# Layer 2 of a sparse graph kernel: row tiles 12 to 20 take two node tiles whole instead of six, and four others through a second list of two chunks

## The chip, the cores and the metric

The kernel runs on one core of a Trainium2 chip. A core has a matrix engine (TensorE, PE in the profile), a vector engine (VectorE, DVE), a scalar engine (ScalarE, ACT), GpSimd (POOL), a queue engine that issues most transfers (SyncE, SP), and 16 DMA engines between its memory (SBUF) and HBM. Each engine works through its own instructions in a fixed order and waits for others by semaphores. The metric is the device time of one execution in microseconds (us); the median of several executions is compared.

## The reference

Four layers over a graph of 2708 nodes with 512 features; `adj` is a 2708 x 2708 matrix of floats, most of them zero. Each layer normalizes x, and its result is added to x. Cut to what matters here, layer 2 is:

```python
h = jnp.maximum(_layernorm(x, axis=-1), 0.0)
h = jax.nn.relu(adj @ (h @ W1) + b1)      # first pass over adj
h = jax.nn.relu(adj @ (h @ W3) + b3)      # second pass over adj
x = x + jnp.tanh(h @ Wf + bf)
```

Layer 0 and layer 3 also multiply by matrices made from `adj`. The nodes are drawn so that the first ones have most neighbours: the probability of an entry falls with the square root of both indices. The inputs have a fixed seed.

## The kernel before, in words

The nodes are cut into 22 tiles of 128 (NT = 22; the last has 20). A row tile m is 128 rows of `adj`. Its columns are taken in two ways. The six first node tiles (DENSE = 6, 768 columns, where nearly every column is used) are multiplied whole. Of the other columns only those that have an entry in some row of m are multiplied: layer 0 counts them, finds their indices with a search (line 377) and stores the indices in `idx_g` and the gathered columns of `adj` in `listed[m]` in HBM, in CHUNKS[m] chunks of 128. Row tiles 12 to 20 have 6, 6, 6, 5, 6, 5, 5, 5 and 5 chunks. Row tile 0 has none; it takes all columns whole.

Layer 2 goes twice through all row tiles, in the loops at lines 1039 (first pass, source g1d in HBM) and 1208 (second pass, source g2d, where tile 0 comes first, then 6 to 20 with the last tile among them, then 1 to 5). For each row tile, `aggregate` (line 905) accumulates in two PSUM banks:

- For the whole tiles it loads three node tiles of `adj` at a time (`load_piece`), splits each piece into a high part (ACT, line 933), a low part and a mixed part (DVE, 934 and 935), and multiplies each node tile in three fast products (line 946) with parts of the features that stay in SBUF.
- For the list it loads `listed[m]` (line 890, two buffers) and gathers the features of each chunk with an indirect transfer from GpSimd (line 897) into one of eight buffers gg0 to gg7, used in turn. Each chunk is one product in full FP32 (line 949), which the engine runs as two passes.
- In the first pass ACT also marks the nonzero entries of whole and listed columns for layer 3 (line 915).

The sum goes through ACT and DVE (lines 823, 824, 974), is transposed on PE (837), split (842, 843, 846) and multiplied by a weight matrix (862). In the first pass the result `go` is stored to g2d; the second pass has a longer tail with tanh, a norm and a second weight product.

The order in which the instructions stand on each engine is fixed by a scheduler before the run; the program's text gives priorities and buffers. Tiles named `slot0` to `slot19` hold x and y while row tile 0 makes its products in the first pass, and the loaded g2 while it does so in the second. Weight banks, `a_hi`, `a_lo`, `a_s` and `ac` have two buffers each.

Of the kernel before, what the change touches and what calls it, by code (L numbers as in the profile page):

```python
# [9 lines left out]
FP = mybir.dt.float32  # L10
# [12 lines left out]
P = 128  # L23
# [12 lines left out]

DENSE = 6
LEAD = 3
CHUNKS = (0, 10, 9, 8, 7, 7, 7, 7, 6, 6, 6, 6, 6, 6, 6, 5, 6, 5, 5, 5, 5, 2)


@with_exitstack
def kernel(
# [43 lines left out]
    def rows(t):  # L87
        return min(P, N - t * P)
# [37 lines left out]
    BEHIND = DENSE * P  # L126
    WIDE, LOW = (N - BEHIND) // 4, BEHIND // 2
    assert WIDE * 4 == N - BEHIND and WIDE < BLK and LOW * 2 == BEHIND
    cnt_b = dram.tile([NGROUP, P, WIDE], BF, name="cnt_b")
    cnt_l = dram.tile([NGROUP, P, LOW], BF, name="cnt_l")  # L130

# [2 lines left out]

    idx = const.tile([P, NT], U32, name="idx")
    BAD_BOUND, BAD_NEG, BAD_MANY = NT, NT + 1, 2 * NT + 1
    bad = const.tile([P, 3 * NT + 1], FP, name="bad")
    nc.gpsimd.memset(bad, 0.0)
    flag = const.tile([P, 1], I32, name="flag")

# [1 line left out]
    idx_g = const.tile([P, NT, NCH], U32, name="idx_g")  # L142

    rdeg = const.tile([P, NT], FP, name="rdeg")
    ones_b = const.tile([P, 1], BF, name="ones_b")
    nc.gpsimd.memset(ones_b, 1.0)

# [69 lines left out]
    with tc.tile_pool(name="l0_slab", bufs=2) as slabs, tc.tile_pool(  # L217
# [29 lines left out]
        nc.gpsimd.iota(place_i, pattern=[[P, NCH]], base=1, channel_multiplier=1)  # L247
        places = hp.tile([P, NCH], FP, name="places")
        nc.vector.tensor_copy(places, place_i)

        pending, pending_c = [], []

# [547 lines left out]
    NGG = 8  # L800
# [12 lines left out]
    NMARK = DENSE + NCA  # L813
    gather_slot = [0]

    def gathered():
        name = f"gg{gather_slot[0] % NGG}"
        gather_slot[0] += 1
        return gp.tile([P, D], FP, name=name)

    def sum_banks(dst, main, mixed, n):

# [63 lines left out]
        return raw[:k, : len(ts), :n], k  # L886

    def load_listed(m):
        ac = ap.tile([P, NCA, P], FP, name="ac")[:, : CHUNKS[m], : rows(m)]
        nc.sync.dma_start(out=ac, in_=listed[m])  # L890
        return ac

    def gather(m, gd, gs=None, index=idx_g):

# [10 lines left out]
    def aggregate(m, parts, shifted, gd, marked):  # L905


        n = rows(m)
        whole, num = dense_of(m), CHUNKS[m]
        if marked:  # L910
            nz = ap.tile([P, NMARK, P], U8, name="nz", bufs=3)

            def mark(i, a):
                k, ts = a.shape[:2]
                nc.scalar.activation(nz[:k, i : i + ts, :n], a, AF.Sign)
        main = ps_a.tile([P, D], FP, name="agg") if dense_of(m) else None
        mixed = ps_a.tile([P, D], FP, name="aggs")
        chunks = []
        if num:
            ac = load_listed(m)  # L920
            chunks = [(ac[:, c, :], g) for c, g in enumerate(gather(m, gd))]
            if marked:
                mark(whole, ac)
        for ts in dense if dense_of(m) else []:
            gs = [parts(t) for t in ts]
            raw, k = load_piece(m, ts)
            hi, lo, s = (
                ap.tile([P, PIECE, P], FR, name=f"a_{part}") for part in ("hi", "lo", "s")
            )
            d = (slice(0, k), slice(0, len(ts)), slice(0, n))  # L930
            if marked:
                mark(ts[0], raw)
            nc.scalar.activation(hi[d], raw, AF.Copy, scale=UP)  # L933
            nc.vector.tensor_tensor(lo[d], raw, hi[d].bitcast(FP), ALU.subtract)  # L934
            nc.vector.scalar_tensor_tensor(
                s[d], lo[d].bitcast(FP), SHIFT, hi[d].bitcast(FP), op0=ALU.mult, op1=ALU.add
            )
            for i, t in enumerate(ts):
                ghi, glo, gs_ = gs[i]
                first, last = t == 0, t == DENSE - 1  # L940
                for acc, a, b, st, sp in (
                    (main, hi, ghi, first, False),
                    (main, lo, glo, False, last),
                    (mixed, s, gs_, first, False),
                ):
                    nc.tensor.matmul(acc[:n], a[:k, i, :n], b[:k], start=st, stop=sp)  # L946
        if chunks:
            for c, (a, g) in enumerate(chunks):
                nc.tensor.matmul(  # L949
                    mixed[:n],  # L950
                    a,
                    g,
                    start=(c == 0 and not dense_of(m)),
                    stop=(c == len(chunks) - 1),
                )
        else:
            for ts in others:
                gs = [shifted(t) for t in ts]
                raw, k = load_piece(m, ts)
                for i, t in enumerate(ts):  # L960
                    nc.tensor.matmul(
                        mixed[:n], raw[:, i, :], gs[i][:k], start=False, stop=(t == NT - 1)
                    )
        if marked:
            nc.sync.dma_start(out=nonzero[m], in_=nz[:, : whole + num, :n])
        return main, mixed
# [69 lines left out]
    w3 = split_w(wsetb, wr, "wb")  # L1036
    wr = load_w(wset, wf_d, "wr")

    for m in order_m:
        n = rows(m)  # L1040
        parts = aggregated(m, first_parts, first_product, g1d, bias1, marked=True)
        if m == 0:
            wf = split_w(wset, wr, "wa")
# [163 lines left out]
    FIRST = 2  # L1207
    for m in order_2:
        n = rows(m)
        parts = aggregated(m, second_parts, second_product, g2d, bias3)  # L1210
        if m == 0:
            w = split_w(wsetb, wr, "wb")
# [499 lines left out]
```

## Time and profile before

| | |
|---|---|
| median of 9 runs | 1487.31 us (1481.0 to 1492.78) |
| profiled execution | 1489.11 us, span of the profile 1487.3 us |
| mean granted PE clock | 0.94 |
| layer 2, list products of line 949 | first at 646.2 us, last at 1269.6 us |
| whole products, line 946 | 3 groups of 252, mean 457, 405 and 401 ns |
| list passes, line 949 | 520, mean 597 ns |
| gathers, line 897 | 130 in each pass, mean 1023 and 1008 ns |
| DMA | 351.27 MB, 236 GB/s over the span |

Times of matmuls are from start to an estimated end and overlap when they follow each other closely; the spacing of their starts is what they cost. Idle time of an engine is given with what ended it. In a row of a timeline the columns are start, duration, engine, line, operation, output and inputs, count, and in brackets the idle time before it. A wait names who waited, for whom, total us, times, and the longest.

### The profile page before, as it was taken

The page shows a single profiled execution, that of the slowest core. Times are in us where ns is not written, and L with a number is a line of the kernel's source. Part 1 is how long each engine was busy: PE and PEld are TensorE (multiplying, and loading weights), DVE is VectorE, ACT ScalarE, POOL GpSimd, SP SyncE. Part 2 cuts the span into 40 slices and gives each one's busy share as a digit, 9 for nine tenths or more (in the row PEclk, how much of TensorE's full clock was granted, in tenths as well). Part 3 has the DMA queues.
Part 4 walks back from the last instruction along what each step waited for, and adds up shares of the span by engine and source line. Part 5 has one row for each costly group of instructions (what it writes and reads, how often), then busy time and mean ns, then how long its engine had stood idle before and what let it go on. Part 6 is the DMA issues. An engine that isn't in the chain of part 4 may idle for free. (4 is left out here: it accounts for less than half of the span.)

```text
span 1487.3 us, 15398 instructions
## 1 busy us (share of the span) xinstructions
PE 1306.7 (88%) x4400; PEld 771.2 (52%) x4400; DVE 939.5 (63%) x1888; ACT 676.4 (45%) x1040; POOL 672.8 (45%) x690
## 2 busy tenths in 40 slices
PE   6487889789778769999999999899999999768997
PEld 2133434334333246655656666565676666556664
DVE  2577879779879679543344446465666665565574
ACT  5987555374111256432333334254445444454453
POOL 1172657667553332055544441234324345157762
PEclk9698989999889879999999999999999999889998
DMA  8998989997786597377777777756555666377884
GB/s 294 307 344 289 332 286 308 311 288 219 224 327 227 147 319 242 103 232 259 247 239 223 235 223 236 240 155 200 178 170 161 210 195 204 102 259 247 263 260 144
DMA packets 195940, 351.27 MB, mean 236 GB/s; under 512 B 26444, under 2 KB 107692, under 8 KB 192113
## 3 DMA queue, kind: packets, MB, share of 16 engines
q1 hardware_dynamic: 148453, 200.68, 40.5%
q0 software_dynamic: 47392, 149.51, 32.3%
q8 instruction: 37, 0.61, 0.2%
q14 instruction: 58, 0.48, 0.1%
HBM read 286.99 MB, written 63.12 MB: 235 GB/s over the span
## 5 line engine op out<-in xcount | busy, mean ns | idle before, releaser
L949 PE MATMUL aggs<-gg,ac 128*128 128x512 f32 (+1 forms) x520 | 233.7, 597 | 3.8 <-DMA gg<-g1d,idx_g 3.8
L897 POOL DMA_INDIRECT gg<-g2d,idx_g x130 | 131.0, 1008 | 218.7 <-PE aggs L949 169.8
L897 POOL DMA_INDIRECT gg<-g1d,idx_g x130 | 133.0, 1023 | 174.9 <-PE aggs L949 104.4
L741 PE MATMUL acc<-h,inc 128*128 128x512 f32 x348 | 165.7, 618 | 29.4 <-DVE inc L600 26.3
L532 POOL DMA_INDIRECT ac<-in_adj_t_dram,idx_a x130 | 131.6, 1012 | 85.2 <-issue 32.3
L949 PEld LDWEIGHTS aggs<-gg,ac 128*128 128x128 f32 (+1 forms) x520 | 98.0, 190 | 111.5 <-issue 102.5
L550 POOL DMA_INDIRECT h<-h0d,idx_g x111 | 113.4, 1021 | 89.9 <-PE acc L741 62.9
L741 PEld LDWEIGHTS acc<-h,inc 128*128 128x128 f32 x348 | 64.8, 196 | 108.1 <-issue 67.8
L946 PE MATMUL agg<-ghi,a_hi 128*128 128x512 f32 x252 | 115.2, 457 | 5.0 <-ACT a_hi L933 4.7
L933 ACT ACTIVATE a_hi<-raw 128x384 fp32r<-128x384 f32 x84 | 43.5, 519 | 161.5 <-issue 89.0
L741 PE MATMUL acc<-h,incl 128*128 128x512 f32 (+1 forms) x222 | 105.2, 620 | 0.0
L946 PE MATMUL agg<-glo,a_lo 128*128 128x512 f32 x252 | 102.1, 405 | 1.8 <-ACT glo L200 1.8
L946 PE MATMUL aggs<-gs,a_s 128*128 128x512 f32 x252 | 100.3, 401 | 0.7 <-DVE gs L197 0.6
L897 POOL DMA_INDIRECT gg<-hidr,idx_h x79 | 78.2, 990 | 46.0 <-PE agg L1133 15.5
L934 DVE TENSOR_TENSOR a_lo<-raw,a_hi 128x384 fp32r<-128x384 f32 x84 | 47.2, 562 | 79.9 <-ACT a_hi L933 53.6
L157 PE MATMUL yacc<-wvo,hT 128*128 128x512 f32 (+1 forms) x176 | 87.3, 642 | 3.9 <-ACT hT L186 3.8
L843 DVE SCALAR_TENSOR_TENSOR v_lo<-pt,v_hi 128x512 fp32r<-128x512 f32 (+1 forms) x88 | 56.7, 664 | 46.5 <-ACT v_hi L842 45.9
L824 DVE SCALAR_TENSOR_TENSOR u<-aggs,u 128x512 f32<-128x512 f32 x42 | 28.8, 687 | 77.5 <-PE aggs L949 75.9
L741 PEld LDWEIGHTS acc<-h,incl 128*128 128x128 f32 (+1 forms) x222 | 43.6, 200 | 53.8 <-issue 50.1
L483 ACT ACTIVATE sgn<-ar 128x2708 bf16<-128x2708 f32 (+1 forms) x22 | 54.0, 2455 | 36.1 <-DMA ar<-in_adj_dram 35.5
L842 ACT ACTIVATE v_hi<-pt 128x512 fp32r<-128x512 f32 (+1 forms) x88 | 48.8, 578 | 44.5 <-PE pt L837 42.6
L514 DVE FIND_INDEX8 at_top<-top,ar 128x8 uint32<-128x2708 f32 (+1 forms) x22 | 65.3, 2969 | 0.0
(275 smaller groups left out, 2776.9 us busy)
## 6 DMA issues: line engine op xcount, KB each, us to landing
ar<-in_adj_dram SPq DMA_DIRECT2D x27, 1354.0 KB
raw<-in_adj_t_dram SPq DMA_DIRECT2D x108, 192.0 KB
slot<-x SPq DMA_DIRECT2D x41, 256.0 KB
at<-in_adj_t_dram SPq DMA_DIRECT2D x27, 384.0 KB
ranks<-rank_b SPq DMA_DIRECT2D x20, 485.0 KB
ac<-lst SPq DMA_DIRECT2D x16, 384.0 KB
h<-in_x_dram SPq DMA_DIRECT2D x21, 256.0 KB
h0d<-h POOLq DMA_DIRECT2D x21, 256.0 KB, 7.1
```

The lines of the kernel that those rows point to most:

```text
L157: nc.tensor.matmul(acc[:n], hT[:, c, :n], w[:, c, :], start=(c == 0), stop=(c == NCD - 1))
L483: nc.scalar.activation(sgn[:n], ar[:n], AF.Sign, accum_out=sum_sgn[:n])
L514: nc.vector.max_index(at_top[:n], top[:n], ar[:n])
L532: nc.gpsimd.indirect_dma_start(out=ac[:, c, :n], out_offset=None, in_=adj_units, in_offset=bass.IndirectOffsetOnAxis(ap=idx_a[:, m, c0 + c ...
L550: nc.gpsimd.indirect_dma_start(out=g, out_offset=None, in_=h0d[:, :], in_offset=bass.IndirectOffsetOnAxis(ap=idx_g[:, m, c : c + 1], axis=0),)
L741: nc.tensor.matmul(acc[:n], a, g, start=(i == 0), stop=(i == len(pairs) - 1))
L842: nc.scalar.activation(hi[d], pt[d], AF.Relu, scale=UP)
L843: nc.vector.scalar_tensor_tensor(lo[d], pt[d], 0.0, hi[d].bitcast(FP), op0=ALU.max, op1=ALU.subtract)
L897: nc.gpsimd.indirect_dma_start(out=gs[c], out_offset=None, in_=gd[:, :], in_offset=bass.IndirectOffsetOnAxis(ap=index[:, m, c : c + 1], ax ...
L934: nc.vector.tensor_tensor(lo[d], raw, hi[d].bitcast(FP), ALU.subtract)
L946: nc.tensor.matmul(acc[:n], a[:k, i, :n], b[:k], start=st, stop=sp)
L949: nc.tensor.matmul(mixed[:n], a, g, start=(c == 0 and not dense_of(m)), stop=(c == len(chunks) - 1),)
```

## The change

For row tiles 12 to 20 (`is_sparse`), in both passes, only node tiles 0 and 1 are multiplied whole (FEW = 2). The columns of node tiles 2 to 5 (512 of them) are searched for those that are used, and taken as two more chunks (FEW_CHUNKS = 2). The columns of `adj` for these chunks are gathered straight from the transposed input into the free end of the `ac` tile, twice, once in each pass; with the two gathers of features that makes four more transfers from GpSimd per row tile and pass.

The search runs in the first pass: `few_ranks` once, before row tile 4, makes running counts for nine row tiles from the counts of layer 0, and `few_search` for row tile m runs in the iteration of row tile m - 6. Its indices go to unused places in `idx_g`. If more than 256 columns are used, a flag leads to the general path, as with the other list.

The first pass still loads all six whole tiles, because it marks them for layer 3; the second pass does not load what it does not use. Gathered features may use slot1 to slot4 besides gg0 to gg7: in the first pass from row tile 1 on, in the second for row tiles from 6 on.

```diff
+SPARSE, FEW, FEW_CHUNKS = 12, 2, 2
...
+    rank_f = dram.tile([NT, (DENSE - FEW) * P], HF, name="rank_f")
...
+        nc.vector.tensor_copy(places_f, places[:, :8])
...
+    more_places = [[]]
+
     def gathered():
-        name = f"gg{gather_slot[0] % NGG}"
+        names = [f"gg{i}" for i in range(NGG)] + more_places[0]
+        name = names[gather_slot[0] % len(names)]
         gather_slot[0] += 1
         return gp.tile([P, D], FP, name=name)
...
+    FEW_A, FEW_G = max(CHUNKS[SPARSE:]), max(CHUNKS[SPARSE:]) + FEW_CHUNKS
+    BETWEEN = (DENSE - FEW) * P
...
+    def is_sparse(m):
+        return SPARSE <= m < NFULL
+
+    def few_ranks():
+        r = NFULL - SPARSE
+        total, rank = (
+            ap.tile([P, PIECE, P], FR, name=f"a_{part}").rearrange("p t k -> p (t k)").bitcast(to)
+            for part, to in (("hi", BF), ("lo", HF))
+        )
+        for g in range(r // GROUP):
+            nc.sync.dma_start(
+                out=total[g * GROUP : (g + 1) * GROUP, : DENSE * P].rearrange(
...
+        rank = rank[:r, :BETWEEN]
+        nc.vector.tensor_scalar_min(rank, total[:r, FEW * P : DENSE * P], 1.0)
+        nc.vector.tensor_tensor_scan(rank, rank, rank, 0.0, ALU.add, ALU.max)
+        nc.sync.dma_start(out=rank_f[SPARSE:NFULL], in_=rank)
+
+    def few_search(m):
+        ranks = ap.tile([P, PIECE, P], FR, name="a_s").rearrange("p t k -> p (t k)").bitcast(HF)
+        nc.sync.dma_start(
+            out=ranks[:, :BETWEEN], in_=rank_f[m : m + 1].to_broadcast([P, BETWEEN])
+        )
...
+        nc.vector.tensor_scalar_add(end, ranks[:, BETWEEN - 1 : BETWEEN], 1.0)
+        nc.vector.tensor_copy(ranks[:, BETWEEN:], end)
+        nc.vector.tensor_scalar(want, places_f, end, None, op0=ALU.min)
+        nc.vector.max_index(at, want, ranks)
...
     def load_listed(m):
-        ac = ap.tile([P, NCA, P], FP, name="ac")[:, : CHUNKS[m], : rows(m)]
-        nc.sync.dma_start(out=ac, in_=listed[m])
-        return ac
+        ac = ap.tile([P, NCA, P], FP, name="ac")[:, :, : rows(m)]
+        nc.sync.dma_start(out=ac[:, : CHUNKS[m]], in_=listed[m])
+        return ac[:, : CHUNKS[m]], ac[:, FEW_A : FEW_A + FEW_CHUNKS]
+
+    def gather_few(m, gd, ac):
+        gs = [gathered() for _ in range(FEW_CHUNKS)]
+        for dst, src, i in [(ac[:, c, :], adj_units, FEW_A + c) for c in range(FEW_CHUNKS)] + [
+            (g, gd[:, :], FEW_G + c) for c, g in enumerate(gs)
+        ]:
+            nc.gpsimd.indirect_dma_start(
+                out=dst,
+                out_offset=None,
+                in_=src,
+                in_offset=bass.IndirectOffsetOnAxis(ap=idx_g[:, m, i : i + 1], axis=0),
+            )
+        return [(ac[:, c, :], g) for c, g in enumerate(gs)]
...
+        taken = whole
+        if is_sparse(m):
+            taken = FEW
+            chunks += gather_few(m, gd, ac_few)
+        for ts in dense if whole else []:
+            if not marked:
+                ts = [t for t in ts if t < taken]
+                if not ts:
+                    continue
+            raw, k = load_piece(m, ts)
+            if marked:
+                mark(ts[0], raw)
+            ts = [t for t in ts if t < taken]
+            if not ts:
+                continue
+            raw = raw[:, : len(ts)]
             gs = [parts(t) for t in ts]
-            raw, k = load_piece(m, ts)
...
-                first, last = t == 0, t == DENSE - 1
+                first, last = t == 0, t == taken - 1
...
-    for m in order_m:
+    for i, m in enumerate(order_m):
         n = rows(m)
+        more_places[0] = [f"slot{i}" for i in range(1, 5)] if m else []
+        if m == SPARSE // 2 - 2:
+            few_ranks()
+        if is_sparse(m + SPARSE // 2):
+            few_search(m + SPARSE // 2)
...
+        more_places[0] = [f"slot{i}" for i in range(1, 5)] if m >= DENSE else []
         parts = aggregated(m, second_parts, second_product, g2d, bias3)
```

## The prediction

> **What bounds the kernel now.** I read the page first: engine shares, then the 40 slices.
>
> ```profile
> PE 1306.7 (88%) x4400; PEld 771.2 (52%) x4400; DVE 939.5 (63%) x1888; ACT 676.4 (45%) x1040; POOL 672.8 (45%) x690
> ...
> PE   6487889789778769999999999899999999768997
> ...
> DMA  8998989997786597377777777756555666377884
> ```
>
> An average of 88% says little, but slices 17 to 34 (about 640 to 1270 us) are layer 2, and there TensorE stands at 9 nearly throughout, with DMA at 5 to 7. The changed row tiles, 12 to 20, are run once in each pass. From the times at which their list products start, they fill about 797 to 913 us in the first pass and 1036 to 1180 us in the second. I asked for the busy time of every engine in two stretches inside them (columns: PE, PEld, DVE, ACT, POOL busy, granted clock, DMA share, GB/s):
>
> ```profile
> 780.00:895.00 115.00, 114.56 (x416) 72.14 (x415) 50.31 (x83) 38.73 (x73) 51.93 (x51) 1.00 0.72 229
> 1040.00:1176.00 136.00, 135.47 (x534) 92.54 (x534) 87.67 (x163) 67.98 (x103) 51.01 (x51) 1.00 0.57 179
> ```
>
> TensorE is idle for 0.4 and 0.5 us. Its waits between 720 and 905 us are one line:
>
> ```profile
> PE main L862 <- ACT go L830: 1.3, 1, 1.3
> ```
>
> So here TensorE is the bound, at full clock, and what a row costs is its matmul pitch, from start to start. The order of work on PE, where row 15 begins its list:
>
> ```profile
> 847.64 0.39 PE L946 MATMUL aggs<-gs,a_s 128*128 128x512 f32 x1
> 847.87 4.45 PE L949 MATMUL aggs<-gg,ac 128*128 128x512 f32 x10
> 851.76 0.80 PE L946 MATMUL agg<-ghi,a_hi 128*128 128x512 f32 x1
> 852.39 0.40 PE L946 MATMUL agg<-glo,a_lo 128*128 128x512 f32 x1
> ```
>
> The reader should see that durations overlap: a whole-tile product (L946) is issued every 0.23 us, not every 0.40. A list product runs as two passes, ten passes for row 15's five chunks in 3.89 us: 0.39 us a pass, 0.78 us a chunk. The first L946 after a list takes 0.63 us, 0.40 more than the others: a switch price. Rows follow each other every 12.9 us with six chunks (783.36 to 796.27) and 12.0 with five (847.87 to 859.86): the nine rows take 4 x 12.9 + 5 x 12.0 = 111.6 us. In the second pass a row takes 16.0 or 15.1 us.
>
> GpSimd, which issues the gathers, is the one to watch:
>
> ```profile
> 865.25 0.95 POOL L897 DMA_INDIRECT gg<-g1d,idx_g  x1 [0.30 <-PE aggs L949]
> 866.51 1.01 POOL L897 DMA_INDIRECT gg<-g1d,idx_g  x1 [0.31 <-issue]
> 867.82 0.95 POOL L897 DMA_INDIRECT gg<-g1d,idx_g  x1 [0.30 <-PE agg L946]
> 874.06 1.17 POOL L897 DMA_INDIRECT gg<-g1d,idx_g  x1 [5.29 <-PE aggs L949]
> ```
>
> A gather is 0.95 to 1.2 us and 0.30 us of issue; 51 of them were busy 51.93 us above, so 1.02 + 0.30 = 1.32 us each. Today GpSimd then waits 5.3 us a row for a freed buffer.
>
> **What the Trainium skill says.** "DMA: Bandwidth & Descriptors", section "Anatomy of one DMA — SWDGE (gpsimd) path", prices a transfer from GpSimd at 2.0 us plus bytes over 436 GB/s, mostly completion latency: 2.6 us for 256 KB, an estimate. The trace has 3.2 to 5.7 us, median 4.4, in the first stretch; I use 4.4. "TensorE: Matmul & The Clock Gate", section "Weight-path perf modes — Fast Weight Load (FWL) and DoubleRow", excludes FP32 from fast weight loads. The trace shows 189 ns for list weights and 188 for the others, and both lie under matmuls, so I charge weights nothing.
>
> **The change, part by part.**
>
> *Whole products removed.* Four tiles of six, three products each: 12 x 0.23 = 2.75 us per row and pass. Also gone are two thirds of the splitting on ACT and DVE (0.52 us on ACT, 0.56 twice on DVE, per piece), worth nothing while TensorE is the bound; and in the second pass 256 KB of raw loads per row. The first pass still loads them, for the marks.
>
> *List products added.* Two chunks, four passes of 0.39: 1.57 us. A chunk thus costs more than a whole tile's three products (0.78 against 0.69); the gain is that two chunks stand for four tiles. Net 1.18 us per row and pass; 18 of these are 21.2 us, the most this mechanism can give.
>
> *Order on TensorE.* The changed order in the first pass puts one or two list products of the next row ahead of the weight product of this one, as filler for the wait on the transpose. That makes two returns from list to other products instead of one: 0.40 back, 0.78 net, 9 x 0.78 = 7.0 us. In the second pass this holds for two rows and the other seven have one return: 2 x 0.78 + 7 x 1.18 = 9.8. But there the transposes and the weight product now follow with no whole product between; v_hi (about 0.6 us on ACT) comes out some 0.3 us late: minus 2. I take 8.
>
> *Gathers.* Four more per row and pass: 49 listed ones become 85 for the nine rows, 85 x 1.32 = 112 us against TensorE's 111.6 - 7 = 104.6. GpSimd would be the longer one in the first pass. What covers it is its lead: 12 buffers instead of 8, and adjacency gathers that need no gg buffer, so it may be about 8 gathers, 10 us, ahead when row 12 starts, and 112 - 10 = 102. That is no margin, and the transfers grow too: the DMA engines are busy 0.72 x 115 / 9.2 rows = 9.0 us a row. Two gathers of 256 KB (64 packets of 4 KB, 208 ns, over 16 engines: 0.83 us) and two of 64 KB (0.25 us) add 2.2: 11.2 us in a row of 11.2 to 12.1. I leave 2 of the 7 us to late gathers: 5. Without the lead, nothing is left of the first pass. In the second pass a row needs 10 x 1.32 = 13.2 us of 14.8, and the DMA share stays near 0.7: covered.
>
> *Search.* Nine max_index over 513 values; the layer 0 row has 2172 ns for 1941, so 0.6 us, and eight small operations of 0.15 to 0.2: 2 us each on DVE. They stand between v_s and the sum of go, where DVE idles 1.8 us, and the next split is needed 4 us later: hidden, I charge 0.5 in all. Below nothing is excluded. If the ranks' load were late, DVE would hold everything behind it: 9 x 2 = 18 us with no cover. The load stands behind the list load on SP; the whole tile's split behind it still has those 4 us. The ranks themselves (three small loads, two operations on nine partitions, one store) happen once, in the same cover.
>
> *The end of the first pass.* slot1 to slot4 hold gathered rows until rows 19 and 20 use them; only then can g2 of nodes 1 to 4 be loaded there for the second pass. Before, those loads were early. On ACT and DVE the split of g2 now stands ahead of v_hi and v_lo of row 19, which feed a weight product. A landing of 3 to 5 us against 2.9 us of cover gives 0 to 5 us; I take 2.
>
> Sum against the profiled execution (span 1487.3, total 1489.1): -5 - 8 + 2 + 0.5 = -10.5, so 1478.6; against the median of nine, 1487.3, which it exceeds by 1.8: 1477.
>
> **Rivals.** (1) Full gain: the lead holds, DVE and DMA stay ahead: -7 - 9.8 to -21, 1466 to 1470. For: TensorE's idle time of 0.4%. Against: gathers and DMA both within a few per cent of the row time. (2) Given back: first pass no faster (112 us of gathers, no lead), boundary 5, search 1: -8 + 6, about 1486. For: the arithmetic above without the buffers; against: around 655 us GpSimd already issues nine in a row at 1.25 us. (3) Slower: gathers become the bound of the first pass at a longer pace, because the DMA engines are full. With the lead of 10 us, TensorE's loss there is 85p - 10 - 111.6; it eats the 6 us of the second pass after the boundary at p = 1.50 us. At 1.65 us it is +18.7 - 6, 1500. For: DMA at 11.2 of some 11.5 us; against: slices with DMA at 9 and 344 GB/s exist, and at 650 to 700 us the pace stayed at 1.25 with DMA at 0.78. (4) The change does not do what it says: a row tile with over 256 used columns among the four tiles raises the flag and starts the general path. The inputs have at most 239 (row 14): excluded.
>
> **How the numbers follow.** Likeliest, TensorE-bound with part of the first pass lost, 0.45: 1477, itself 1470 to 1482. Full gain 0.20: 1468. Given back 0.18: 1486. Slower 0.17: 1500. Faster by 0.3% (below 1482.8, about what this kernel's measurement can tell) is 0.65, within it 0.18, slower 0.17. For 8 in 10 the range runs from 1465 to 1494, leaving out the upper part of the slow case and a little below full gain.
>
> **What would show it.** Right: 216 whole products fewer and 72 list passes more at unchanged pitch; rows 13 to 20 of the second pass at about 14 to 15 us; in the first 11.3 to 12.3 us, with TensorE waiting on gg gathers for a few us in the last rows; GpSimd without its 5 us pauses. Wrong: TensorE waiting on DVE in rows 6 to 14 (search), on v_lo around 900 us by more than 5 us, or list products waiting on every row.

## The result, and the profile after

The changed kernel takes 1504.84 us (median of 10 runs, 1496.54 to 1517.79) against 1487.31 us: ratio 1.0127, 95% interval 1.010 to 1.0154. It is slower. The forecast was 1477 with a range up to 1494. The profiled execution took 1502.54 us, its span is 1500.8 us.

From the page of the changed kernel, engine shares and slices (same columns as for the kernel before):

```profile
PE 1302.8 (87%) x4256; PEld 750.6 (50%) x4256; DVE 933.3 (62%) x1945; ACT 665.5 (44%) x1022; POOL 738.6 (49%) x762
...
PE   6487989789778679999989998899999999778996
...
PEclk9698999999889889999999998999999999989998
...
DMA  8998999987695587287868886756677667278884
```

TensorE has 144 instructions fewer, as forecast (216 whole products out, 72 passes in), and 4 us less busy time. But the slices of 750 to 788 and of 901 to 938 us, which were nines, are eights. Busy time by stretch (length, then busy time of PE, PEld, DVE, ACT, POOL, then granted clock, DMA share, GB/s), for the forecast's stretch of the first pass, for rows 13 to 20 of the first pass, and inside the second pass:

```profile
780.00:895.00 115.00, 106.80 (x340) 61.77 (x341) 44.22 (x106) 31.01 (x61) 75.72 (x77) 0.95 0.81 253
830.70:938.90 108.20, 95.54 (x296) 56.94 (x295) 40.44 (x67) 31.45 (x60) 55.96 (x57) 0.91 0.77 241
1060.00:1196.00 136.00, 132.87 (x479) 80.95 (x478) 78.41 (x147) 64.08 (x96) 81.31 (x83) 1.00 0.70 218
```

TensorE was busy for 99.6% of the first pass's stretch before (780 to 895 us). Now it is busy for 88% of rows 13 to 20, at a clock of 0.91. What it waits for in the first pass (total us, times, longest):

```profile
PE pt L919 <- DVE u L1082: 9.6, 4, 3.1
PE main L944 <- ACT go L912: 5.3, 1, 5.3
PE main L944 <- ACT v_hi L924: 4.3, 1, 4.3
PE aggs L1057 <- DMA gg<-g1d,idx_g: 3.4, 1, 3.4
```

The gathers (last line) hold it once, at 645 us, before any sparse row. The other three lines are results of ACT and DVE that come late.

To say where the time went I cut layer 2 at five events of the profile: DVE's end of the sum `go` of row tiles 9, 12 and 20 in the first pass, TensorE's end of the second pass's unlisted products (those of row tile 0, which has no list), and the start of its last list product. The short last row tile, 21, runs between 9 and 10. The same cuts serve for all experiments below; each is one execution, in us:

| stretch | before | after | e1 | e2 | e3 | e4 | e5 | e6 | e7 | e9 | e12 |
|---|---|---|---|---|---|---|---|---|---|---|---|
| start to row 9 | 778.3 | 780.6 | 777.6 | 783.8 | 781.1 | 779.6 | 784.2 | 779.4 | 782.5 | 784.8 | 777.0 |
| row 9 to row 12 | 43.2 | 50.1 | 48.4 | 48.8 | 50.5 | 48.4 | 43.2 | 43.2 | 50.3 | 43.8 | 50.6 |
| row 12 to row 20 | 99.3 | 108.3 | 97.1 | 96.0 | 107.5 | 94.3 | 99.3 | 91.8 | 87.9 | 91.7 | 90.4 |
| row 20 to unlisted end | 15.2 | 17.6 | 23.2 | 23.8 | 20.5 | 18.5 | 14.8 | 19.0 | 17.2 | 17.2 | 16.9 |
| to the last list product | 334.1 | 330.7 | 330.4 | 328.9 | 332.3 | 330.1 | 335.2 | 330.1 | 329.9 | 330.5 | 329.8 |
| rest | 217.3 | 213.6 | 210.5 | 209.4 | 211.6 | 214.8 | 210.7 | 215.8 | 214.3 | 215.6 | 212.7 |

Before to after: +2.3, +6.9, +9.0, +2.4, -3.4, -3.7, in all +13.5, the difference of the spans. The first and the last stretch vary by several us between single executions (e5 has 210.7 us of rest with layer 3 untouched), so I read nothing from them. The loss lies in the first pass: 7 us in rows 10 to 12, of which only row 12 is itself sparse (6.6 of the 7 are lost by row 11's sum, where the search runs beside rows that the change leaves whole), and 9 us in rows 13 to 20, which were to gain 5.

**The loop in the sparse rows.** SP's own queue in the changed kernel (start of the issue, duration), from the store of one row's product to the next:

```profile
859.59 0.34 SPq L1161 DMA_DIRECT2D g2d<-go  x1
866.51 0.34 SPq L1172 DMA_DIRECT2D slot<-g2d  x1
866.95 0.37 SPq L972 DMA_DIRECT2D ac<-lst  x1
872.23 0.32 SPq L1073 DMA_DIRECT2D nz<-nz  x1
872.65 0.94 SPq L962 DMA_DIRECT2D raw<-in_adj_t_dram  x2
874.27 0.34 SPq L1161 DMA_DIRECT2D g2d<-go  x1
```

The second line is the reload of what the first line stores, for the second pass. It needs the store's data in HBM, so SP stands for 6.9 us, and the list load of the next row goes out only then. SP's waits for its own stores over rows 13 to 20, after and then before:

```profile
SPq L1172 <- DMA g2d<-go: 36.4, 7, 6.6
```

```profile
SPq L1059 <- DMA g2d<-go: 3.3, 3, 2.0
```

The same stretch in the kernel before, with another row's loads between:

```profile
859.74 0.32 SPq L1048 DMA_DIRECT2D g2d<-go  x1
861.00 0.38 SPq L880 DMA_DIRECT2D raw<-in_adj_t_dram  x1
861.75 0.32 SPq L1059 DMA_DIRECT2D slot<-g2d  x1
865.20 0.32 SPq L890 DMA_DIRECT2D ac<-lst  x1
```

Here the store has landed after 2.0 us. That an issuing engine has to stand for this is what the Trainium skill states in "DMA: Bandwidth & Descriptors", section "Two DMAs through the same engine are not ordered": a transfer that reads what an earlier one wrote must wait for the earlier one's completion semaphore before it is issued. Both traces agree, 2.0 and 6.9 us.

Two things in the traces could make 2.0 into 6.9 us. The same section says that within one queue of one DMA engine descriptors start in order, and in the changed kernel two raw loads (192 KB each) are issued directly ahead of the store, before only smaller or earlier ones. And the DMA engines are fuller. Here is the time between store and reload in the changed kernel, then in the kernel before (columns as above):

```profile
859.60:866.50 6.90, 5.47 (x13) 3.84 (x14) 3.42 (x6) 0.62 (x2) 5.20 (x6) 0.55 0.92 289
```

```profile
859.70:861.70 2.00, 2.00 (x7) 1.00 (x6) 1.13 (x3) 1.16 (x3) 0.55 (x1) 1.00 0.35 131
```

In the kernel before the store falls into GpSimd's pause: GpSimd is busy for 0.55 us, and the DMA engines for 35% (27 to 36% in five rows). In the changed kernel the gathers go on through it, and the share is 92% (89 to 100% in five rows). No run tests the two apart.

On ACT, which works in its order too, the list load comes late (in brackets the idle time and what ended it):

```profile
862.21 0.60 ACT L924 ACTIVATE v_hi<-pt 128x512 fp32r<-128x512 f32 x1 [2.58 <-PE pt L919]
871.47 0.74 ACT L1011 ACTIVATE nz<-ac 128x640 uint8<-128x640 f32 x1 [8.66 <-DMA ac<-lst]
872.11 0.92 ACT L1011 ACTIVATE nz<-raw 128x384 uint8<-128x384 f32 x2
872.94 0.58 ACT L912 ACTIVATE go<-main 128x512 f32<-128x512 f32 x1
```

ACT's mark of the listed columns waits 8.7 us, and the sum `go`, whose four last products TensorE ran from 867.03 to 868.2 us, stands behind it. `go` is what the next store waits for: store 859.59, reload 866.51, list load 866.95, mark 871.47, `go` 872.94 (then its sum on DVE), store 874.27. That is a loop of 14.7 us through SP, HBM, ACT and DVE, and TensorE's products are no link of it. ACT's wait for the list load over rows 13 to 20, after and then before:

```profile
ACT nz L1011 <- DMA ac<-lst: 46.0, 6, 9.5
```

```profile
ACT nz L915 <- DMA ac<-lst: 9.6, 6, 2.1
```

I call it theory T1 that this loop paces the sparse rows. T2 is that the search does, because DVE stands in its order on the loads of the rank rows; T3 that the gathers do (the forecast's own rival for a slower kernel); T4 that slot1 to slot4, which now also hold gathered rows, come free too late for the second pass.

### The profile page after: what moved, and what is told of

It is laid out like the page before. It is cut to its first block, busy times and chain, and to the rows that moved or that the text cites. A ratio compares the mean times of both kernels' runs of the same rounds, so it can differ in the third digit from the quotient of the medians.

```text
span 1500.8 us, 15329 instructions
## 1 busy us (share of the span) xinstructions
PE 1302.8 (87%) x4256; PEld 750.6 (50%) x4256; DVE 933.3 (62%) x1945; ACT 665.5 (44%) x1022; POOL 738.6 (49%) x762
## 5 line engine op out<-in xcount | busy, mean ns | idle before, releaser
L1057 PE MATMUL aggs<-gg,ac 128*128 128x512 f32 (+1 forms) x424 | 198.4, 603 | 4.3 <-DMA gg<-g1d,idx_g 3.4
L539 POOL DMA_INDIRECT ac<-in_adj_t_dram,idx_a x130 | 130.6, 1005 | 84.3 <-issue 32.9
L993 POOL DMA_INDIRECT gg<-g2d,idx_g x99 | 96.5, 974 | 139.0 <-PE aggs L1057 83.6
L993 POOL DMA_INDIRECT gg<-g1d,idx_g x87 | 90.3, 1038 | 95.4 <-issue 57.4
L1054 PE MATMUL agg<-ghi,a_hi 128*128 128x512 f32 x180 | 85.3, 474 | 5.7 <-ACT a_hi L1041 3.9
L1041 ACT ACTIVATE a_hi<-raw 128x384 fp32r<-128x384 f32 (+1 forms) x66 | 32.2, 490 | 111.7 <-PE agg L1054 74.2
L1057 PE MATMUL aggs<-slot,ac 128*128 128x512 f32 x168 | 77.8, 592 | 0.0
L913 DVE TENSOR_TENSOR go<-mixed,go 128x512 f32<-128x512 f32 (+1 forms) x33 | 22.6, 686 | 84.6 <-ACT go L912 66.1
L1054 PE MATMUL agg<-glo,a_lo 128*128 128x512 f32 x180 | 72.7, 404 | 2.0 <-ACT glo L206 2.0
L1054 PE MATMUL aggs<-gs,a_s 128*128 128x512 f32 x180 | 71.5, 407 | 0.7 <-DVE gs L203 0.6
L748 PEld LDWEIGHTS acc<-h,incl 128*128 128x128 f32 (+1 forms) x222 | 43.2, 198 | 53.2 <-issue 49.4
L944 PE MATMUL main<-wb,v_hi 128*128 128x512 f32 (+1 forms) x176 | 58.6, 458 | 12.0 <-ACT v_hi L924 6.6
```

The lines of the kernel that those rows point to most:

```text
L539: nc.gpsimd.indirect_dma_start(out=ac[:, c, :n], out_offset=None, in_=adj_units, in_offset=bass.IndirectOffsetOnAxis(ap=idx_a[:, m, c0 + c ...
L748: nc.tensor.matmul(acc[:n], a, g, start=(i == 0), stop=(i == len(pairs) - 1))
L944: nc.tensor.matmul(acc[:n], a[:, c, :n], b[:, c, :], start=first and c == 0, stop=last and c == NCD - 1,)
L993: nc.gpsimd.indirect_dma_start(out=gs[c], out_offset=None, in_=gd[:, :], in_offset=bass.IndirectOffsetOnAxis(ap=index[:, m, c : c + 1], ax ...
L1057: nc.tensor.matmul(mixed[:n], a, g, start=(c == 0 and not dense_of(m)), stop=(c == len(chunks) - 1),)
```

## Experiments

The experiments ran in five groups, each on one chip and next to the kernel before. e1 to e4 ran beside a median of 1487.42 us for it, e5 to e8 beside 1485.66, e9 to e12 (same chip as e5 to e8) beside 1486.31. The last two groups fell on other chips, where the kernel before takes 1523.10 us (e13 to e15) and 1525.96 us (e16 to e18); their times are only compared within their group.

### One part at a time: e1, e2, e3

```diff
-        if is_sparse(m):
+        if False:                          # e1
+        if is_sparse(m) and not marked:    # e2
+        if is_sparse(m) and marked:        # e3
             taken = FEW
```

> The ranks, the search and the four further gather buffers stay; both passes take six node tiles whole, as the kernel before. Theory T1 (the loop store of g2d, reload on SP, listed load, ACT's mark, next store paces the sparse rows of the first pass) puts nothing here but asks that the search rows keep their own loss. Theory T2 (DVE stands on the ranks' loads in rows 6 to 14) expects 5 to 9 us over the kernel before, with g2d's store of row 12 at 827 to 831 us and of row 20 about 99 us later. Theory T3 (GpSimd's gathers bound the sparse rows) expects no loss here, under 2 us. Theory T4 (slots 1 to 4 come free too late at the start of the second pass) expects 2 to 4 us from the boundary alone.

> Search and buffers stay; only the second pass is sparse, the first takes six node tiles whole. By T1 and T2 together: the first pass costs the search alone (+5 to +9), the second gains 3 to 8, so -3 to +6 us against the kernel before, and the first pass from row 12 to row 20 takes 99 us again. If the sparse second pass itself lost time, this would be slower than the run with the search alone.

> Search and buffers stay; only the first pass is sparse, the second takes six node tiles whole. T1 expects the whole loss of the changed kernel and more, because the gain of the second pass (3 to 8 us) is missing: 18 to 26 us over the kernel before, row 12 to row 20 at about 108 us. If the loss came from the second pass or the boundary, this would be within 8 us of the kernel before.

Measured: e1 1495.43 us, ratio 1.0048 (1.0033 to 1.0063); e2 1493.31 us, 1.0033 (1.0012 to 1.0054); e3 1501.89 us, 1.0082 (1.0038 to 1.0127).

What is there only to prepare the sparse rows costs 7 to 8 us by itself (e1, by the ratio and by the medians): 5.2 in rows 10 to 12 and 8.0 at the start of the second pass, more than the 2 to 4 that T4 gave it, of which other stretches give some back. The sparse second pass (e2) is no loss; against e1 it gains 2 us by the medians, inside the error. The sparse first pass loses: its rows 13 to 20 take 107.5 us in e3, 97.1 in e1. e3 as a whole loses 14.5 us by the medians, less than the 18 to 26 that T1 expected. DVE's wait for the ranks in e1, from 745 to 830 us (row 12 ends at 826):

```profile
DVE few_small L873 <- DMA a_s<-rank_f: 20.7, 6, 4.3
```

### The reload taken out of the loop: e4, e5

```diff
-        go = wp.tile([P, D], FP, name="go")
+        stay = 5 <= m < NSLOT
+        go = gp.tile([P, D], FP, name=f"slot{m}") if stay else wp.tile([P, D], FP, name="go")
+        if stay:
+            g2[m] = go                     # the second pass reads it there
         sum_banks_scaled(go, main, mixed, n)
         nc.sync.dma_start(out=g2d[span(m)], in_=go[:n])
```

The store to g2d stays, because the gathers read it. e4 is the changed kernel with this edit; SP's order in rows 13 to 17 is otherwise the same. e5 is the kernel before with it.

> The changed kernel, with one edit: rows 5 to 19 of layer 2's first pass write their product straight into the buffer that the second pass reads, so that the reload from DRAM behind the store falls away; 15 SP loads fewer, the rest of SP's order is the same. T1 expects row 12 to row 20 to fall from 108 us to 93 to 98 and the kernel to gain 9 to 14 us on the changed one (1491 to 1496). T3 (gathers bound these rows) expects no gain there, 1503 to 1506. T2 expects rows 9 to 12 unchanged, g2d's store of row 12 at 829 to 832.

> The kernel before with the same edit as e4 alone: rows 5 to 19 write straight into the second pass's buffer, 15 reloads fewer. In the kernel before the reload is issued 2 to 3 us after the store and nothing waits for it on the path, so T1 expects next to nothing: 1484 to 1489, row 12 to row 20 at 98 to 99.5 us. If the reload cost the kernel before as much as the changed one, 1470 to 1476, and e4 would say nothing about the change.

Measured: e4 1486.93 us, ratio 0.9996 (0.9975 to 1.0016); e5 1483.17 us, 0.9993 (0.9974 to 1.0013). Rows 13 to 20 fall from 108.3 to 94.3 us in e4 and stay at 99.3 in e5. e4 gains more than T1 expected, about 18 us on the changed kernel, and the reload costs the kernel before nothing that can be measured. The changed kernel's SP and ACT in e4:

```profile
862.20 0.34 SPq L1165 DMA_DIRECT2D g2d<-slot  x1
866.37 0.34 SPq L972 DMA_DIRECT2D ac<-lst  x1
```

```profile
ACT nz L1011 <- DMA ac<-lst: 9.6, 6, 2.0
```

The list load goes out 4.2 us after the store, not 7.4, and now it is TensorE, still reading the buffer, that it waits for. The mark's wait is back at the 9.6 us of the kernel before. Row tiles 13 to 17 fill this stretch of e4:

```profile
828.00:884.70 56.70, 56.70 (x188) 33.00 (x187) 21.54 (x35) 17.84 (x35) 43.08 (x45) 1.00 0.90 274
```

TensorE is busy without a break, at full clock. T1 is shown: the reload on SP is what turned the sparse first pass from a gain of 5 us over the kernel before (99.3 to 94.3) into a loss of 9. The edit takes out SP's wait and 256 KB of transfers a row together, and no run has one without the other. But the DMA engines are as busy in this stretch of e4 (0.90) as in the changed kernel from 830.7 to 886.4 us (0.88), so the waits point to SP and not to the transfers.

### Which link closes the loop: e11

ACT's mark of the listed columns reads a weight tile of the same size in place of the list load, so layer 3's masks for these columns are not made from `adj`.

```diff
             if marked:
-                mark(whole, ac)
+                filled = w3[0].bitcast(FP).rearrange("p c d -> p (c d)")
+                mark(whole, filled[:, : num * n].rearrange("p (c k) -> p c k", c=num))
```

> The changed kernel with its reloads on SP, but ACT's mark of the listed columns reads a weight tile that is long there instead of the listed load (so layer 3 gets wrong masks for these columns, with the same work on ACT). T1 says that ACT standing in its order on the listed load is the link that closes the loop: row 12 to row 20 should fall from 108 us to 94 to 100 and the kernel to 1488 to 1496. If the list products on TensorE, which wait for the same load, close it as well, the rows stay at 104 or more and the kernel at 1500 or more.

Measured: 1508.68 us, ratio 1.015 (1.0111 to 1.0189); rows 13 to 20 in 103.3 us. The expectation of T1 failed here: the list load is not the one link. ACT's longest wait in these rows is now another mark's:

```profile
ACT nz L1011 <- DMA raw<-in_adj_t_dram: 38.2, 7, 8.7
```

The raw loads of the whole tiles, which the first pass still takes for the marks, stand behind the same reload:

```profile
859.44 0.32 SPq L1173 DMA_DIRECT2D slot<-g2d  x1
859.93 0.32 SPq L972 DMA_DIRECT2D ac<-lst  x1
860.34 0.54 SPq L962 DMA_DIRECT2D raw<-in_adj_t_dram  x1
...
865.54 0.52 ACT L1011 ACTIVATE nz<-raw 128x384 uint8<-128x384 f32 x1 [8.71 <-DMA raw<-in_adj_t_dram]
865.97 0.58 ACT L912 ACTIVATE go<-main 128x512 f32<-128x512 f32 x1
```

A wait took the place of the one removed. Rows 13 to 15 still take 15.0 to 15.8 us each; in rows 16 to 18, at 10.6 to 10.8, the loop is gone though the reload is there. So the loop's fixed part is SP's stand on its own store, and different loads behind it can close it.

### The gathers: e12

e4 without the two adjacency gathers per sparse row of the first pass; the two new chunks use the listed chunks' columns there a second time.

```diff
-        for dst, src, i in [(ac[:, c, :], adj_units, FEW_A + c) for c in range(FEW_CHUNKS)] + [
+        for dst, src, i in [
+            (ac[:, c, :], adj_units, FEW_A + c) for c in range(FEW_CHUNKS) if gd is not g1d
+        ] + [
```

> e4 without the two adjacency gathers of the first pass's sparse rows (the two new chunks use the listed chunks' columns there, so layer 2 comes out wrong): GpSimd has two gathers of 1.25 us less per row, TensorE the same products. T3 (gathers are the next bound of these rows once the loop is gone) expects row 12 to row 20 to fall from 94 us by 3 or more and the kernel to 1480 to 1484. If TensorE or its waits on ACT and DVE bound them, the rows stay within 1.5 us and the kernel at 1485 to 1488.

Measured: 1478.49 us, ratio 0.9947 (0.9899 to 0.9995). Rows 13 to 20 take 90.4 us against 94.3 in e4, the 3 us or more that T3 expected. But row by row this is not T3: rows 13 to 18 take 67.5 us in both, and all of the difference lies in rows 19 and 20 (26.9 us in e4, 22.9 in e12). In rows 13 to 17 of e4 TensorE never stopped, as shown above, with all the gathers there. So with the loop gone the gathers do not bound these rows, TensorE does. In rows 19 and 20 ACT waits for slot1 to slot4 to be reloaded for the second pass, 6.3 us in e4 and 2.7 in e12; the gathers may delay these reloads, but no run tests that.

### The search: e6, e9, e10

e6 loads the rank rows early into free slots, e10 loads each into the ring of gather buffers. e9 is e4 without ranks and search; in their place it copies four index columns of the listed chunks, so the new chunks gather rows that have nothing to do with the search in both passes.

```diff
-        ranks = ap.tile([P, PIECE, P], FR, name="a_s").rearrange("p t k -> p (t k)").bitcast(HF)
+        ranks = gp.tile([P, D], FP, name=f"slot{m - 1}").bitcast(HF)   # e6, loaded in few_load(m)
+        ranks = gathered().bitcast(HF)                                 # e10
...
-            few_ranks()                                                # e9, few_search too
+            nc.vector.tensor_copy(idx_g[few + (slice(FEW_A, FEW_A + 4),)], idx_g[few + (slice(0, 4),)])
```

> e4, and the rank rows are loaded one row ahead or earlier into buffers that are still free (slot11 to slot19), not into the ring of a_s just before the search. T2a (DVE stands in its order on late rank loads) expects row 9 to row 12 to fall from 48.4 us to 43 to 45 and the kernel to 1482 to 1484. T2b (the search's own 2 us a row on DVE, or the traffic of the loads, costs it) expects row 9 to row 12 to stay at 47 to 49 and the kernel at 1486 to 1488.

> e4 without ranks and search: in their place one copy fills the index columns from the listed chunks' own (so both passes gather rows of no meaning for the two new chunks). The whole price of the search is the difference to e4. T2 expects row 9 to row 12 at 42 to 44 us and the kernel at 1480 to 1483; if the rows 9 to 12 lose their time to something else (the four further buffers, slots 1 to 4), they stay at 47 to 49 and the kernel at 1486 to 1488.

> e4, but the rank rows are loaded into the gather buffers' ring in place of the ring of a_s: the load goes out ahead of the list's load, and stays one per row, not bunched as in e6. T2a (DVE stands on late rank loads) expects row 9 to row 12 at 43 to 45 us and 1482 to 1485. T2b (2 us of search a row on DVE) expects 47 to 49 and 1486 to 1489.

Measured: e6 1489.56 us, ratio 1.0038 (1.0019 to 1.0056); e9 1485.15 us, 0.9985 (0.9946 to 1.0023); e10 1499.19 us, 1.0091 (1.0044 to 1.0139).

Rows 10 to 12 take 43.8 us without the search and 48.4 with it: 4.6 us, against 0.5 forecast. T2's range for the whole kernel, 1480 to 1483, was missed all the same, and the intervals of e4 and e9 overlap. In the changed kernel DVE's lines show why:

```profile
807.08 0.15 DVE L873 TENSOR_SCALAR few_small<-a_s 128x1 f32<-128x1 f16 x1 [2.93 <-DMA a_s<-rank_f]
...
807.68 0.69 DVE L876 FIND_INDEX8 few_found<-few_small,a_s 128x8 uint32<-128x513 f16 x1
...
809.06 0.68 DVE L906 SCALAR_TENSOR_TENSOR u<-aggs,u 128x512 f32<-128x512 f32 x1
809.77 0.69 DVE L1082 TENSOR_TENSOR u<-u,bias 128x512 f32<-128x512 f32 x1
```

The first operation waits 2.9 us for the ranks, the search takes 2.0 us more, and `u`, which TensorE's transpose needs, stands behind both. The search's own size was right; the wait in front of it was not priced.

Neither repair worked. In e6 rows 10 to 12 are down to 43.2, but with all ranks there the scheduler put all nine searches into rows 3 and 4 (682 to 704 us), and rows 1 to 9 take 135.1 us (779.4 - 644.3, row 0 to row 9) where e4 takes 126.2. Its profile is also its shortest run of 20, so the table flatters it; its median is 2.6 us over e4's, on another chip. In e10 DVE stood even longer, 34.5 us over the nine searches against 24.0 in e4. Six of the nine make the line below, the other three 7.5 us:

```profile
DVE few_small L873 <- DMA gg<-rank_f: 27.0, 6, 6.6
```

So the cost moves with the search, and I have no version in which it disappears. T2a was expected to show in e10's rows 10 to 12 and did not: 52.5 us.

### The boundary and both repairs: e7, e8

Rows 0 to 19 keep their product in place, slot1 to slot4 are no gather buffers in the first pass, slot16 to slot19 are in rows 1 to 14. e8 has e6's early ranks too.

```diff
-        more_places[0] = [f"slot{i}" for i in range(1, 5)] if m else []
+        more_places[0] = [f"slot{i}" for i in range(16, 20)] if 0 < m < 15 else []
...
-        stay = 5 <= m < NSLOT
+        stay = 0 <= m < NSLOT
```

> e4, but rows 0 to 19 all write straight into the second pass's buffers, slot1 to slot4 are no gather buffers in the first pass, and slot16 to slot19 are in their place in rows 1 to 14 only. T4 (slots 1 to 4 come free and are loaded too late) expects the time from row 20's product to the end of the second pass's first unlisted products to fall from 18.5 us to 13 to 16, the kernel to 1482 to 1485. If the boundary is bound by something else (the gathers, the raw loads), it stays at 18 or more and the kernel at 1486 to 1490.

> e6 and e7 together (rank rows in slot7 to slot15). T2a and T4 add up: 1476 to 1481, faster than the kernel before by 0.4 to 0.7%. If either fails, 1481 to 1487.

Measured: e7 1484.83 us, ratio 0.9992 (0.9973 to 1.0011); e8 1488.17 us, 1.0018 (1.0002 to 1.0035). In e7's profile rows 13 to 20 take 87.9 us, 11.4 less than before, but rows 10 to 12 take 50.3, and the boundary 17.2 against 18.5 in e4. T4 expected 13 to 16 there. Its cost stands one stretch earlier: row 19 alone takes 16.5 us in e4 and 11.6 in e7, and from row 18's sum to the end of the unlisted products e4 takes 45.4, e7 39.0 and the kernel before 39.7. e7 has other gather buffers too, so of these 6.4 us an unknown part, at most all, is the sharing's; the medians do not show it. e8's 1488.17 lies above both of its expectations. Neither version beats the kernel before by what can be measured.

### Buffers or search, and two other chips: e13 to e18

e13 is the kernel before with the four further buffers alone, e14 is e1 with eight buffers. e15 is e7 without ranks and search (as e9).

> The kernel before with the four further gather buffers (slot1 to slot4) and nothing else: six whole tiles, no ranks, no search. If T4 (the sharing of slots 1 to 4) makes the loss of e1, 1490 to 1495; if the search makes it (T2), 1485 to 1489, with row 9 to row 12 at 43 us as before.

> e1 with eight gather buffers: ranks and search alone, added to the kernel before, their results unused. T2 expects most of e1's loss here: 1490 to 1495, row 9 to row 12 at 47 to 49 us. T4 expects 1486 to 1489.

> e7 without ranks and search (the two new chunks take the listed chunks' indices, so their rows have no meaning): sparse rows in both passes, no reload, no search, no sharing of slots 1 to 4. If loop, search and sharing are all that the forecast missed, this shows its gain: 1474 to 1479. If the gathers and the waits of the sparse rows hold back most of it, as e9 and e12 suggest, 1481 to 1486.

Measured, against 1523.10 us: e13 1533.98, ratio 1.0064 (1.003 to 1.0098); e14 1524.00, 1.001 (0.9986 to 1.0035); e15 1577.74, 1.0354 (1.0276 to 1.0432).

With six whole tiles the buffers cost more than the search, contrary to what I had taken from e1. The profiles agree on the places: the boundary takes 23.4 us with the buffers (e13) and 17.4 without (e14), rows 10 to 12 take 50.2 us with the search and 43.1 without. How e14 makes up for its rows 10 to 12 stays open; there is no trace of the kernel before from that chip.

e15 was meant to show what the sparse rows are worth without loop and search. Instead it lost 3.5%, so e16 and e17 are e7's and e15's kernels again, side by side on one more chip, and e18 is e15's without the first pass's adjacency gathers.

> The kernel of e7, as the reference of this call: 0.2% within the kernel before.

> The kernel of e15 (no reload, no search, indices of no meaning for the two new chunks). If loop and search are all that the forecast missed: 8 to 10 us below the kernel before and 6 or more below e16. If gathers and waits hold back the rest: 2 to 5 us below e16.

> e17 without the two adjacency gathers per sparse row of the first pass (the listed chunks' columns are used twice there; layer 2 has no meaning). If GpSimd's gathers bound the sparse rows of the first pass, 3 us or more below e17; if TensorE's own waits do, within 1.5 us of it.

Measured, against 1525.96 us: e16 1573.44, ratio 1.0333 (1.0287 to 1.0378); e17 1576.33, 1.0372 (1.0318 to 1.0426); e18 1552.28, 1.018 (1.0121 to 1.0238). The kernel that is level with the one before on one chip is 3.3% slower on another, itself slower by 2.7%. e16's second pass takes 358.3 us where e7's takes 329.9. The kernels with six whole tiles take 335.9 and 336.6 (e13, e14) on the chip of e13 to e15, and e15's second pass 365.6 there. One row of the second pass, from row tile 14's sum to row tile 15's, in e16 and then in e7 (columns as above):

```profile
1165.50:1185.70 20.20, 17.91 (x57) 9.89 (x56) 8.91 (x18) 7.25 (x11) 11.03 (x12) 0.94 0.60 183
```

```profile
1102.40:1118.70 16.30, 15.75 (x56) 9.40 (x55) 9.05 (x18) 7.76 (x12) 11.46 (x12) 1.00 0.83 266
```

The same products and gathers in 20.2 and 16.3 us, with fewer bytes per us. e18 says what is sensitive in the first pass: without 18 adjacency gathers, rows 13 to 20 take 87.9 us instead of 103.5 (e17) and the kernel is 24 us faster; in e12, beside e4, they gave 3.9 us in rows 19 and 20 and some 7 in the kernel, each taken against the kernel before beside it. Why these gathers cost more there isn't settled: part of TensorE's waits in e16's second pass is put down to nothing that the trace shows:

```profile
PE main L944 <- issue: 8.6, 9, 2.3
```

So what the sparse rows would be worth with loop, search and sharing all gone was not measured on a chip like the first three; e9 (1485.15) and e7 (1484.83) bound it only in part.

## Why the prediction was wrong, step by step

**The change on TensorE: right in counts, one price misread.** The instruction counts came out as forecast. A list pass costs 0.43 us between starts, not 0.39: the median is 0.429 in every stretch of both kernels that I took (67 to 126 pairs each). The 3.89 us I divided by ten hold nine steps, and the 0.40 "switch price" is the rest of the tenth pass, since the product after a list is recorded 0.03 us after the last pass begins. So a chunk costs 0.86 us and returning from a list costs nothing extra. Net per row and pass that is 2.75 - 1.72 = 1.03 us, and 18.6 us for the whole change instead of 21.2; the 0.78 a row that I took for the first pass, with two returns, falls with the switch price.

**"-5" for the first pass: the step that failed.** It was +9 in rows 13 to 20. The step *Gathers* asked what GpSimd and the DMA engines would do, and nothing asked what SP would: its wait for its own store was put at nothing, and measured 36.4 us. The order of SP's instructions shows the reload directly behind its store, with two raw loads in front and the list load behind it. In the kernel before, the reload stands there as well and costs nothing (e5). My reading, which no run tests alone: there the store landed after 2 us, in GpSimd's pause, and 18 whole products a row gave the loads behind it time to land; the change left six of these products, put the raw loads in front of the store and filled the pause with gathers. The forecast had named the end of these pauses as a sign of being right.

With the reload gone (e4) the rows take 94.3 us, a gain of 5.0: the very size that I had forecast, but by other terms. Rows 13 to 18 gain 7.2 us, the full 6 x 1.03 and a little more, so the TensorE bound and the gathers' lead held; rows 19 and 20 lose 2.3, to the waits told under "+2" below. The 2 us put aside for late gathers met no late gather: in rows 13 to 20 no list product of the changed kernel waits for one.

**"0.5" for the search: failed.** It was 6.9 us in rows 10 to 12 (4.6 by e4 and e9). The sentence that DVE would hold everything behind it if the ranks' load were late was true, and I set its price (up to 18 us) beside a cover that I did not check: the load goes out late on SP (in the row shown at 802.25 us, behind a store and not behind the list load), and in rows 8 to 12 it lands up to 3.0 us after DVE arrives.

**"+2" at the end of the first pass: the right wait, the number by luck.** The wait that I named came in row 19, before the stretch that the table gives for this place:

```profile
921.48 0.63 ACT L196 ACTIVATE ghi<-slot 128x512 fp32r<-128x512 f32 x1 [5.53 <-DMA slot<-g2d]
922.01 0.58 ACT L924 ACTIVATE v_hi<-pt 128x512 fp32r<-128x512 f32 x1
922.64 2.08 PE L944 MATMUL main<-wb,v_hi 128*128 128x512 f32 x4 [4.31 <-ACT v_hi L924]
```

ACT stands 5.5 us on a reloaded slot, v_hi stands behind it, and TensorE waits 4.3 us: inside my 0 to 5, and part of the +9. The +2.4 of the table's own stretch is something else: there TensorE waits 2.6 us for the raw loads of the unlisted products, before 1.0. With six whole tiles and twelve buffers that stretch costs 8 (e1; e13 has nearly the same length), which I had not asked.

**"-8" for the second pass: -3.4.** The direction was right, the size under half. From row 12 to row 20 of the second pass the products alone give 8 x 1.03 = 8.2. From DVE's sum `u` of row 12 to that of row 20 the traces have 130.6 us before and 127.2 after; e1 and e3, whose second pass is whole, have 130.5 and 130.6, e2 and e4 127.6 and 127.2. So the sparse rows do gain, 3.4 us, and 4.8 come back. The waits seen there are small:

```profile
PE agg L1054 <- ACT u L905: 1.5, 5, 0.3
PE main L944 <- ACT v_hi L924: 1.2, 5, 0.3
```

Counting from start to start, a transpose is followed by the weight product after 0.52 us instead of 0.11 in five rows, and the next row's first whole product comes 0.47 us late in five: 4.4 us. That is the wait on v_hi which I put at 2, and one on the sum `u`, which frees the PSUM bank, which I did not see.

**The rivals.** Rival 3 named 1500 us, near the result, for a reason that is not the one shown. Its premise came true between store and reload, where the DMA engines were 89 to 100% busy, but list products never waited for gathers in the sparse rows of the changed kernel. A rival "SP's queue becomes the bound of a row" was missing, though the kernel's own chain of store and reload was in the trace. Of the signs that I had named for a wrong prediction, TensorE waiting on DVE in rows 6 to 14 came true (2.2 and 1.5 us). v_lo around 900 us did not, but v_hi, which stands beside it, held TensorE for 4.3.

## What to carry to other kernels

Before shortening one engine's part of a row, close the row's other loops on paper: follow each store to its reload, to the loads queued behind it, to the in-order engine that waits for them, and back to the store, and compare that length with the new row time. When the change also fills a pause of another engine, ask what used that pause: here it was the store's landing. A reload of data that the kernel has just had in SBUF can be left out where a buffer is free to take the result at once; that cost nothing here and was worth 18 us on the changed kernel. And a late load in front of a small operation on an in-order engine costs what stands behind it, so price the wait and not only the operation.

## What the runs showed of the hardware

- A product that runs as two passes has its passes 0.429 us apart, a fast product 0.23 us; the product after a list is recorded as starting 0.03 us after the last pass starts, so durations of single rows mislead and distances between starts do not.
- A store of 256 KB took 5.1 to 6.9 us until the reload that waits for it could be issued, in five rows of the changed kernel, with two loads of 192 KB right ahead of it and the DMA engines 89 to 100% busy. In the kernel before it took 2.0 us in the row shown and at most 3.0 in four others, at 27 to 36%.
- In rows 13 to 20 of the changed kernel TensorE stood idle for 3.1, 3.0 and 4.3 us (ending at 861.0, 903.0 and 922.6 us). Each time its granted clock fell to 0.50 before the idle time was over and stayed there for some 6.8 us, as in the line below; the mean of these rows is 0.91. In the first of these stretches four products with v_hi took 2.67 us, in e4 1.20 us. So in these three cases a wait cost more than its length.

```profile
860.30:867.10 6.80, 6.07 (x15) 4.25 (x16) 2.75 (x5) 0.60 (x1) 5.28 (x6) 0.50 0.87 273
```

- Chips differ by more than this change: the kernel before took 1486 to 1487 us in three groups of runs on two chips and 1523 and 1526 us on two others. The kernel of e7, level with it on one of the first (0.9992), lost 3.3% on one of the second (e16). Which part of the chip makes it is open.
